# Two-layer sequence model on one core: attention's first queries and keys in other memory, four heads to a transfer, and one store moved to GpSimd's queue

## Chip, core and metric

The kernel runs on one core of a Trainium2 chip. The metric is the device time of one execution in microseconds (us), the median of several runs. Engines are named as the profile names them: PE (TensorE matmul), PEld (its weight load), DVE (VectorE), ACT (ScalarE), POOL (GpSimd), SP (SyncE, which here only issues transfers). "SPq", "ACTq" and "POOLq" are those engines issuing a transfer.

## What is computed

Input: 8 batches of 512 tokens, 256 wide, float32 throughout. Two layers, each a mixer and an expert feed-forward side by side on the normed input, added to the residual:

```python
x  = L0_attn_u                                   # [8, 512, 256]
xn = layernorm(x)
x  = x + state_space_mixer(xn) + moe_top1(xn)    # layer zero: 8 heads, chunks of 128; 8 experts
xn = layernorm(x)
x  = x + attention(xn) + moe_top2(xn)            # layer one
```

Layer one's attention has 16 heads of width 16 and keys and values that go through a latent of 64:

```python
q = x @ Wq;  latent = (x @ Wk + x @ Wv) @ W_down_kv
k_rec = latent @ W_up_k;  v_rec = latent @ W_up_v
scores = (q_h @ k_h.T) * scale * exp(-0.0001 * |i - j|)      # each batch, each head: 512 x 512
out = softmax(scores) @ v_h ; out @ Wo
```

Its feed-forward has 7 experts of capacity 512 and a "no-op" expert; tokens go to the best two.

## The kernel before

**Three stretches.** Layer zero's mixer goes through 64 chunks (`Chunk`, eight to a batch), with the batch's projections, convolutions and output (`Batch`) cut in pieces between them, and layer zero's experts and then layer one's preparation (`late`: norm, transposes, projections to q, k and v) threaded in by `fill`. Then layer one runs 128 attention steps (`Step`: batch b, group g of four heads, quarter c of the keys), with expert pieces between them. The third stretch, at the end, adds everything up. All instructions are written in a fixed order (`manual_schedule`); each engine runs its own list in order, and a transfer waits on the engine that issues it until what it needs is there, with all that stands behind it in that engine's list.

**The seam.** The last batch of layer zero ends with four calls of `Batch.output` (L1088 to L1102). For the last batch the sum goes into the tile `final` (taken from the tag `xr`), so that layer one can norm it without loading it again; after the fourth piece SP stores it to the DRAM array `x1` (L1100). The projections had put q and k of batches 0 to 6 in DRAM as `rows["q"]` and `rows["k"]`, 256 rows (16 heads of 16) by 512 tokens. In layer one's block, `spread` brings them back for batch 0: one tile of 128 partitions for each group of four heads, head i at partitions 32*i to 32*i+15, one transfer of 16 rows (32 KB) for each head. q goes through SP's queue, k through ACT's (L1728 to L1732); behind them SP loads `vt` (values) and `w_o`. POOL clears `low` and three tiles `wv` (L1739 to L1742). For batches 1 to 7, `inputs_of` (called at step (2,0) of the batch before) loads `vt` at once and puts the 32 transfers in the list `loads`, of which `load_some(6)` in each step hands six to SP.

A score step multiplies four heads at once: `s_ps` (L1580), four matmuls with 16 rows each in four row groups of the array, then DVE takes each through the decay band and its maximum (L1583, `s`), ACT takes the exponentials (L1593, L1597), and two steps later PE multiplies with the values (L1605, `o_ps`). The quotient of a pair of groups goes through DRAM (`divide`: stores `od`, loads `sm` and `oT`, store `rd`, load `rb`, then DVE multiplies at L1723), all on SP's queue. DVE also norms the last batch and builds the routing table of the last batches (`en_r`, `en_b`, `en_w`, L219 to L223), which PE sums up (`tab`, L231).

**Memory.** Tiles come from pools, and a pool from a stack; a tag's buffers lie side by side, and the tags of a pool follow one another in the order in which they are first asked for. Layer zero's pools are closed ahead of layer one's, and the framework puts in the waits that the reuse needs. In bytes of a partition:

| pool | from | to | what lies there |
|---|---|---|---|
| layer zero `m1` | 48608 | 79328 | z, states st0 (56800 to 58848) and st1, x, au, u (71136 and 75232, 4096 each) |
| layer zero `m2` | 79328 | 181920 | yT (79328 and 87520, 8192 each), bc (95712 and 103904, 8192 each), xT (112096 and 116192, 4096 each), the eight `row` buffers (from 120288), mt, fr, xdt and smaller ones |
| layer one `a1` | 53344 | 69440 | w_o, peaks, low (57440 to 57568), wv, rows, oT |
| layer one `a2`, before | 69440 | 132480 | vt (69440), qT (78144, six of 2048), kT (90432, six), s1 (102720, twelve of 2048), then ng, w, sm, fo and smaller ones |
| layer one `a2`, changed | 69440 | 132480 | s1 (69440, twelve), fo (94016, two of 1024), qT (96064, six), kT (108352, six), vt (120640), then the rest |

The tiles of the last batch in layer zero are the second buffers of yT (87520) and u (75232) and the first of bc (95712).

Of the kernel before, what the change touches and what calls it, by code (L numbers as in the profile page):

```python
# [9 lines left out]
FP = mybir.dt.float32  # L10
# [7 lines left out]
P = 128  # L18
B, S, DM = 8, 512, 256
NT = B * S  # L20
NTILE = NT // P
TPB = S // P
# [23 lines left out]
AH, AD, DL = 16, 16, 64  # L46
VH = AD + 1
VW = AH * VH
# [16 lines left out]
def tile_kernel(ctx: ExitStack, tc: tile.TileContext, t, out: bass.AP):  # L65
    nc = tc.nc
    V, A, G, T, Y = nc.vector, nc.scalar, nc.gpsimd, nc.tensor, nc.sync
# [7 lines left out]
    def load(name, shape, pool=None):  # L75
        w = ctile("w_" + name, shape, pool=pool)
        Y.dma_start(out=w, in_=t[name])
        return w
# [35 lines left out]
    x1 = dram.tile([NT, DM], FP, name="x1", tag="x1")  # L114
# [7 lines left out]
    def rows_of(src, b):  # L122
        return src[b * S : (b + 1) * S, :].rearrange("(c p) d -> p c d", p=P)
# [248 lines left out]
    def bank(name, shape, tag="gen"):  # L372
        return mp.tile(shape, FP, name=name, tag=("e", "s")[tag] if isinstance(tag, int) else tag, bufs=2)
# [194 lines left out]
    with ExitStack() as es:  # L568
        p1, p2, psum = m1, m2, mp
# [365 lines left out]
        class Batch:  # L935
# [152 lines left out]
            def output(self, c):  # L1088
                op = bank("op", [P, DM])
                for k in range(HC):  # L1090
                    T.matmul(  # L1091
                        op, self.yT[:, k, c * P : (c + 1) * P], w_out[:, k, :], start=(k == 0), stop=(k == HC - 1)
                    )

                def add():
                    x = self.u[:, c, :]
                    to = final[:, c, :] if self.b == B - 1 else x
                    V.scalar_tensor_tensor(to, op, self.rs[:, c : c + 1], x, ALU.mult, ALU.add)
                    if c == TPB - 1:
                        Y.dma_start(out=rows_of(x1, self.b), in_=final if self.b == B - 1 else self.u)  # L1100

                return add  # L1102

# [122 lines left out]
        with tc.manual_schedule(engines=ENGINES):  # L1226

            rows, rest, sizes = itertools.chain(route0(), blocks()), late(), step_sizes()
# [127 lines left out]
            final = tl.tile([P, TPB, DM], FP, name="xr", tag="xr", bufs=3)  # L1356
# [14 lines left out]
    with tc.tile_pool(name="a1", bufs=1) as p1, tc.tile_pool(name="a2", bufs=2) as p2, tc.tile_pool(  # L1371
        name="ap", bufs=1, space=PSUM
# [80 lines left out]
        def spread(rows, got, n, by=None):  # L1453

            for g in range(4):
                wide = p2.tile([P, S], FP, name=n + "T", tag=n + "T", bufs=6)
                for i in range(4):
                    h = 4 * g + i
                    to, of = wide[32 * i : 32 * i + AD, :], rows[h * AD : (h + 1) * AD, :]
                    if by:  # L1460
                        by.dma_start(out=to, in_=of)
                    else:
                        loads.append((to, of))
                got.append(wide)
# [3 lines left out]
        def load_some(k):  # L1468
            for to, of in loads[:k]:
                Y.dma_start(out=to, in_=of)  # L1470
            del loads[:k]

        def inputs_of(b):
            rows, vd = kept[b]
            got = {"q": [], "k": [], "v": p2.tile([P, TPB, VW], FP, name="vt", tag="vt")}
            Y.dma_start(out=got["v"], in_=vd)
            for n in ("q", "k"):
                spread(rows[n], got[n], n)
            return got
# [68 lines left out]
        def combine():  # L1548


            def add(b):
                G.dma_start(out=x_sb[:, b * TPB : (b + 1) * TPB, :], in_=rows_of(x1, b), accum_op=ALU.add)

            for b in (B - 1, *range(B - 2)):
                add(b)
            yield
            while B - 2 not in finished:
                yield
            add(B - 2)
            for b in range(B - 1):  # L1560
                G.dma_start(out=rows_of(out, b), in_=x_sb[:, b * TPB : (b + 1) * TPB, :])
# [164 lines left out]
                urgent.insert(0, finish(b, oT))  # L1726

        with tc.manual_schedule(engines=ENGINES):  # L1728
            rows, vd = kept[0]
            got = {"q": [], "k": [], "v": p2.tile([P, TPB, VW], FP, name="vt", tag="vt")}  # L1730
            spread(rows["q"], got["q"], "q", Y)
            spread(rows["k"], got["k"], "k", A)  # L1732
            Y.dma_start(out=got["v"], in_=vd)
            w_o = load("w_o", [P, KC, DM], p1)
            steps = [(b, g, c) for b in range(B) for g in range(4) for c in range(TPB)]
# [18 lines left out]
            rows, number1 = combine(), None  # L1754
# [45 lines left out]
            for n in range(N + 2):  # L1800

                if n < N:
                    b, g, c = steps[n]
                    if (g, c) == (2, 0) and b + 1 < B:
                        got = inputs_of(b + 1)
# [15 lines left out]
                    now.scratch = scratch  # L1821
                    done.append(now)
                    now.scores()
                load_some(6)
                for chain in list(chains):
                    if next(chain, "end") == "end":
                        chains.remove(chain)
# [117 lines left out]
def build(arrays):  # L1945
    import concourse.bacc as bacc

    nc = bacc.Bacc("TRN2", target_bir_lowering=False, num_devices=1)
    t = {
        k: nc.dram_tensor(f"in_{k}_dram", v.shape, mybir.dt.from_np(v.dtype), kind="ExternalInput").ap()  # L1950
        for k, v in arrays.items()
    }
    out = nc.dram_tensor("out_0_dram", (NT, DM), FP, kind="ExternalOutput").ap()
    with tile.TileContext(nc) as tc:
        tile_kernel(tc, t, out)
    return nc
# [10 lines left out]
```

## Time and profile before

| what | value |
|---|---|
| three runs | 1734.75 us median, 1732.07 to 1735.76 |
| the profiled execution | 1730.83 us, of which the span is 1729.1 us |
| PE busy | 1567.4 us (91%) |
| DVE busy | 1173.9 us (68%) |
| ACT busy | 916.3 us (53%) |
| POOL busy | 571.0 us (33%) |
| HBM traffic | 133 GB/s over the span |
| q and k loads, all batches | 256 transfers of 32 KB |

All times below are us from the span's start. In the chain of waits, a line is when a piece begins, how long it is on the chain, and what it is; in the timeline, a line is start, duration, engine, source line and what is written from what, with the idle time ahead of it and what ended that in brackets. In tables by stretch, each engine has its busy time, and PEclk is the TensorE clock that was granted, with 1.00 for full speed.

### The profile page before, as it was taken

To read this page: it belongs to the slowest core of one execution; us is meant where nothing else is said; L and a number is where in the kernel's file an instruction comes from. 1 tells how busy PE (TensorE), PEld (TensorE's weight loads), DVE (VectorE), ACT (ScalarE), POOL (GpSimd) and SP (SyncE) were. 2 spreads that over 40 slices of the span, in tenths; PEclk is the share of its full clock that TensorE was granted. 3 is DMA by queue.
4 is the path that set the end of the run, shared out by engine and by line. 5 is a ranking of instruction groups with operands and counts; after the bars stand their busy time and mean duration, and the time that the engine had idled before them with its cause. 6 is when DMAs were issued, how large, how long until landed. Compare 5 with 4: busy or idle time off the path is not lost.

```text
span 1729.1 us, 25738 instructions
## 1 busy us (share of the span) xinstructions
PE 1567.4 (91%) x8700; PEld 962.1 (56%) x8700; DVE 1173.9 (68%) x3067; ACT 916.3 (53%) x2173; POOL 571.0 (33%) x518
## 2 busy tenths in 40 slices
PE   6556799989999999999789898799999999999996
PEld 5323467767677677777445554564455445454442
DVE  6567675575576655875776925657777777777774
ACT  4232345345354453453544643327777777777773
POOL 0041456465465474654532422000211121112030
PEclk9777899999999999999989998759999999999986
DMA  8010445454564564564355624323433343344254
GB/s 295 21 55 0 152 159 198 161 187 180 166 212 146 175 196 148 181 221 137 83 115 163 179 87 145 105 74 114 135 86 111 97 133 97 90 119 141 57 98 125
DMA packets 131821, 231.09 MB, mean 134 GB/s; under 512 B 20109, under 2 KB 93839, under 8 KB 120528
## 3 DMA queue, kind: packets, MB, share of 16 engines
q1 hardware_dynamic: 101952, 119.46, 22.0%
q0 software_dynamic: 28656, 108.69, 20.6%
q8 instruction: 73, 1.20, 0.3%
q10 hardware_dynamic: 1072, 1.18, 0.3%
q14 instruction: 68, 0.56, 0.1%
HBM read 176.75 MB, written 53.58 MB: 133 GB/s over the span
## 4 chain that ended last, share of the span: by engine, by line
PE 71%; DVE 19%; ACT 4%; DMA 3%; issue 2%; POOL 0%; SPq 0%; ACTq 0%; DVEq 0%; POOLq 0%
PE s_ps L1580 7%; PE pj L946 7%; PE h_ps L640 7%; PE o_ps L1605 7%; PE y_ps L664 7%; PE e_hp L1423 5%; PE e_yp L1436 5%; DVE cv L959 3%; PE yd L1172 3%; PE op L1091 3%; PE seg L1134 3%; DVE s L1583 3%; PE sp L1202 2%; PE yoff L1190 2%; ACT s L1597 2%
## 5 line engine op out<-in xcount | busy, mean ns | idle before, releaser
L1583 DVE CUSTOM_DVE_ANT_0 s<-s_ps,band 128x512 f32<-128x512 f32 x512 | 323.1, 687 | 148.2 <-PE s_ps L1580 148.2
L1597 ACT ACTIVATE s<-s,ng 128x512 f32<-128x512 f32 x512 | 325.7, 708 | 0.0
L946 PE MATMUL pj<-xT,w_w_in 128*128 128x512 f32 x384 | 197.3, 640 | 9.5 <-DVE cv L959 5.5
L1441 POOL DMA_INDIRECT x<-e_yo,number x28 | 45.0, 1608 | 422.4 <-ACT e_yo L1440 342.2
L1580 PE MATMUL s_ps<-qT,kT 16*128 16x512 f32 x1024 | 166.7, 678 | 4.6 <-DMA kT<-kd 4.6
L959 DVE SCALAR_TENSOR_TENSOR cv<-pj,w_conv_w,cv 128x511 f32<-128x511 f32 (+2 forms) x192 | 143.2, 746 | 22.2 <-ACT cv L955 17.7
L1118 POOL TENSOR_TENSOR au<-da,half 128x512 f32<-128x512 f32 x64 | 76.6, 1197 | 228.7 <-PE seg L1134 156.7
L640 PEld LDWEIGHTS h_ps<-xdT,w 128*128 128x128 f32 x1152 | 138.8, 194 | 19.1 <-issue 18.3
L1605 PE MATMUL o_ps<-s,wv 128*32 128x512 f32 x1024 | 145.4, 640 | 1.2 <-ACT w L1593 1.2
L640 PE MATMUL h_ps<-xdT,w 128*128 128x128 f32 x1152 | 141.9, 277 | 0.5 <-DMA w<-in_w_dram,w_idx 0.5
L664 PE MATMUL y_ps<-w,hT 128*128 128x256 f32 x576 | 138.4, 384 | 0.0
L664 PEld LDWEIGHTS y_ps<-w,hT 128*128 128x128 f32 x576 | 108.3, 193 | 29.9 <-issue 16.1
L946 PEld LDWEIGHTS pj<-xT,w_w_in 128*128 128x128 f32 x384 | 69.8, 200 | 90.5 <-issue 80.1
L1580 PEld LDWEIGHTS s_ps<-qT,kT 16*128 16x128 f32 x1024 | 51.7, 193 | 119.0 <-DVE w L1590 51.1
L1423 PE MATMUL e_hp<-e_xdT,e_w 128*128 128x256 f32 x448 | 113.5, 391 | 3.7 <-ACT fo L1542 1.9
L1436 PE MATMUL e_yp<-e_w,e_hT 128*128 128x256 f32 x448 | 113.4, 392 | 1.5 <-ACT fo L1542 1.5
L1181 DVE TENSOR_TENSOR yT<-yT,yd 128x512 f32<-128x512 f32 (+1 forms) x64 | 43.8, 684 | 100.2 <-PE yd L1172 100.2
L1147 ACT ACTIVATE mt<-seg,mid 64x64 f32<-64x64 f32 x512 | 109.4, 309 | 0.8
L1436 PEld LDWEIGHTS e_yp<-e_w,e_hT 128*128 128x128 f32 x448 | 80.1, 189 | 50.6 <-issue 30.3
L1423 PEld LDWEIGHTS e_hp<-e_xdT,e_w 128*128 128x128 f32 x448 | 82.1, 191 | 40.8 <-ACT s L1597 15.2
L963 ACT ACTIVATE th<-cv 128x512 f32<-128x512 f32 x64 | 40.3, 630 | 116.7 <-DVE cv L959 108.0
L955 ACT ACTIVATE cv<-pj,w_conv_b,w_conv_w 128x512 f32<-128x512 f32 x64 | 49.8, 778 | 87.4 <-PE pj L946 83.4
(341 smaller groups left out, 2818.3 us busy)
## 6 DMA issues: line engine op xcount, KB each, us to landing
ex<-exd SPq DMA_DIRECT2D x96, 128.0 KB
fr<-fdd SPq DMA_DIRECT2D x64, 128.0 KB
e_w<-in_ei_dram SPq DMA_DIRECT2D x7, 1024.0 KB
od<-os SPq DMA_DIRECT2D x28, 256.0 KB
e_w<-in_eo_dram SPq DMA_DIRECT2D x7, 1024.0 KB
vd<-vt SPq DMA_DIRECT2D x16, 272.0 KB
vt<-vd SPq DMA_DIRECT2D x8, 544.0 KB
u<-in_u_dram SPq DMA_DIRECT2D x8, 512.0 KB
```

Source lines behind the costliest of these rows:

```text
L640: T.matmul(hp[:, i, :], w1[:, k * FF + f * P : k * FF + (f + 1) * P], xdT[:, k * P : (k + 1) * P], start=(k == 0), stop=(k == KC - 1),)
L664: T.matmul(yp, hT[f // 4][:, f % 4, :], w2[:, f * DM : (f + 1) * DM], start=(f == 0), stop=(f == FC - 1),)
L946: T.matmul(pj, w_in[:, k, o * P : (o + 1) * P], self.xT[:, k, :], start=(k == 0), stop=(k == KC - 1))
L959: V.scalar_tensor_tensor(cv[:, s:], pj[:, : S - s], conv_w[:, q, 3 - s : 4 - s], cv[:, s:], ALU.mult, ALU.add)
L1118: G.tensor_tensor(self.au, bc(da[:, d, self.i, :], 2, HH), bc(TRI[d], 1, HH), ALU.mult)
L1147: A.activation(mt[lo, over, h], seg[lo, over, h], AF.Exp, bias=mid[lo, self.i, h : h + 1])
L1423: T.matmul(hp, w1[:, k, f * P : (f + 1) * P], xdT[:, k, :], start=(k == 0), stop=(k == KC - 1))
L1436: T.matmul(yp, hT[:, f, c * P : (c + 1) * P], w2[:, f, :], start=(f == 0), stop=(f == FC - 1))
L1580: T.matmul(sp[i], self.k[r, cols], self.q[r, :], start=True, stop=True)
L1583: V.tensor_tensor_reduce(out=self.p[i], in0=sp[i], in1=band[:, at : at + S], scale=1.0, scalar=KEEP, op0=ALU.mult, op1=ALU.max, accum_out= ...
L1597: A.activation(self.p[i], self.p[i], AF.Exp, bias=self.ng[:, i : i + 1])
L1605: T.matmul(op[32 * i : 32 * i + 32, :], self.wv[:, i, :], self.p[i], start=(self.c == 0), stop=(self.c == TPB - 1),)
```

## The change

Three edits. `Batch.output` stores the last batch through POOL's queue instead of SP's. `spread` moves a group of four heads with one transfer: its source walks over 32 rows from each head's first, so that the upper 16 partitions of each strip receive rows of the next head, which no matmul reads; in the last group, where that would run past the array, one transfer moves three heads and another the fourth. That is 10 transfers a batch in place of 32, 256 KB each where they move four heads, 192 KB and 32 KB in the last group; `load_some` hands over two of them a step in place of six. Last, layer one's block asks for twelve tiles of `s1` and two of `fo`, unused, ahead of all others, and for `vt` behind q and k, so that the tags get the places of the table's last row.

```diff
@@ Batch.output, the last piece
-                        Y.dma_start(out=rows_of(x1, self.b), in_=final if self.b == B - 1 else self.u)
+                        if self.b == B - 1:
+                            G.dma_start(out=rows_of(x1, self.b), in_=final)
+                        else:
+                            Y.dma_start(out=rows_of(x1, self.b), in_=self.u)
@@ spread
-                for i in range(4):
-                    h = 4 * g + i
-                    to, of = wide[32 * i : 32 * i + AD, :], rows[h * AD : (h + 1) * AD, :]
+                strips = 4 if g < 3 else 3
+                of = bass.AP(
+                    tensor=rows.tensor, offset=rows.offset + 4 * g * AD * S, ap=[[AD * S, strips], [S, 32], [1, S]]
+                )
+                moves = [(wide[: 32 * strips, :], of)]
+                if strips < 4:
+                    moves.append((wide[96 : 96 + AD, :], rows[DM - AD :, :]))
+                for to, of in moves:
                     if by:
                         by.dma_start(out=to, in_=of)
                     else:
@@ layer one's block
+            for _ in range(12):
+                p2.tile([P, S], FP, name="s1", tag="s1", bufs=12)
+            for _ in range(2):
+                p2.tile([P, DM], FP, name="fo", tag="fo")
             rows, vd = kept[0]
-            got = {"q": [], "k": [], "v": p2.tile([P, TPB, VW], FP, name="vt", tag="vt")}
+            got = {"q": [], "k": []}
             spread(rows["q"], got["q"], "q", Y)
             spread(rows["k"], got["k"], "k", A)
+            got["v"] = p2.tile([P, TPB, VW], FP, name="vt", tag="vt")
             Y.dma_start(out=got["v"], in_=vd)
@@ each step
-                load_some(6)
+                load_some(2)
```

## Prediction

> **What bounds the kernel now.** I read the page's chain first, by engine:
>
> ```profile
> PE 71%; DVE 19%; ACT 4%; DMA 3%; issue 2%; POOL 0%; SPq 0%; ACTq 0%; DVEq 0%; POOLq 0%
> ```
>
> PE carries the end, and transfers hold only 3% of it. The change can pay only where the chain passes through one of its transfers, so I next read the chain in order of time around the seam:
>
> ```profile
> 1098.00 0.98 PE sm L1078 x8
> 1099.10 7.50 issue
> 1106.59 0.36 ACTq L1461
> 1106.99 3.58 DMA kT<-kd
> 1110.59 5.64 PE s_ps L1580 x13
> ...
> 1121.72 0.40 DVE en_w L223
> 1122.16 7.08 PE tab L231 x32
> ```
>
> A load of keys is on the chain for about 4 us. ("issue" for 7.50 us is not idleness: PE ran the 32 matmuls of the last output then, until 1105.99.) The timeline says what the load waited for and who waited behind it:
>
> ```profile
> 1106.03 0.48 DVE L1098 SCALAR_TENSOR_TENSOR xr<-op,rq_r,u 128x256 f32<-128x256 f32 x1 [0.56 <-PE op L1091]
> 1106.55 0.37 SPq L1100 DMA_DIRECT2D x<-xr  x1
> 1106.59 10.16 ACTq L1461 DMA_DIRECT2D kT<-kd  x16
> 1106.63 0.12 POOL L1739 MEMSET low<- 128x32 f32 x1 [16.42 <-DVE xr L1098]
> 1107.08 9.99 SPq L1461 DMA_DIRECT2D qT<-qd  x16
> 1110.59 6.85 PE L1580 MATMUL s_ps<-qT,kT 16*128 16x512 f32 x16 [4.59 <-DMA kT<-kd]
> 1112.66 0.69 DVE L1583 CUSTOM_DVE_ANT_0 s<-s_ps,band 128x512 f32<-128x512 f32 x1 [5.47 <-PE s_ps L1580]
> 1116.80 0.20 ACT L1593 ACTIVATE w<-w 128x4 f32<-128x4 f32 x1 [17.70 <-DMA kT<-kd]
> ```
>
> The last add of layer zero ends at 1106.51. Within 0.12 us of it three queues come free: SP's store, ACT's first k load, POOL's clearing of `low`. Then all of PE, DVE and ACT wait for the first q and k. The rest of layer one I read by stretches and by the waits of 1200 to 1660:
>
> ```profile
> 1108.50:1110.00 1.50, 0.00 (x0) 0.00 (x0) 0.00 (x0) 0.00 (x0) 0.00 (x0) 0.50 0.86 260
> 1200.00:1600.00 400.00, 396.89 (x2348) 197.96 (x2340) 295.05 (x1080) 306.49 (x634) 64.48 (x48) 1.00 0.38 112
> PE e_hp L1423 <- ACT fo L1542: 1.9, 7, 0.5
> DVE s L1583 <- PE s_ps L1580: 113.0, 99, 3.2
> DVE oT L1723 <- DMA rb<-rd: 2.1, 2, 1.3
> ```
>
> From 1200 to 1600 PE idles 3.1 us in 400, and none of it is charged to q or k; DVE idles on PE. Loads of later batches are hidden.
>
> **Edit one, the memory.** What it could bring: in the old places qT begins inside u's second buffer and kT inside yT's, both used until the very end; in the new ones they lie over bc and xT, last read by PE at 1082.70 (yoff) and about 1084.9 (the last z projection). ACT's list is free from 1099.09 (end of L286) and SP's from about 1099.7. If waits went by bytes, q and k would land before PE's last output matmul.
>
> I don't expect it, because of `low`. It lies at 57440, over state st0, which PE last read (yoff) by 1082.70; no other layer-zero tile shares those bytes. Yet POOL, idle for 16.42 us, was let go by the add that reads `u`, 17 KB further up in the same pool. So reuse is not waited for byte by byte but pool by pool. The program's own waits say the same: its first k transfer waits for the load and the accumulation into `u` and for ACT's copy L1073 into a `row` buffer, none of which shares a byte with it. The edit leaves qT and kT in pool `a2`, which reaches over `m1` and `m2` before and after alike. The last user of both is that add. So ACT's first k load still goes at 1106.59, and SP's first q load, now without the store ahead of it, at about 1106.6. Gain: 0.
>
> **Edit two, four heads to a transfer, first batch.** SP's 16 issues and ACT's 16 become 5 each. What decides is when the first group has landed. Nearest row: rb, 256 KB into 128 partitions, issued alone at 1205.20, let DVE start at 1209.28, 4.08 us later.
>
> ```profile
> 1205.20 0.61 SPq L1720 DMA_DIRECT2D rb<-rd  x1
> 1209.28 0.69 DVE L1723 TENSOR_TENSOR oT<-oT,rb 128x512 f32<-128x512 f32 x1 [1.33 <-DMA rb<-rd]
> ```
>
> That gives 1106.59 + 4.08 = 1110.67, against 1110.59: +0.1. From above: if the second 256 KB (k beside q) came wholly after the first, at the 260 GB/s of the stretch above, 1.0 us more: +1.1. From below: rd, 16 KB, took 3.18 us on the chain (1202.00), so 1106.59 + 3.2 = 1109.8: -0.8; the 512 KB store no longer runs ahead of q on SP's queue, which speaks for that side. I take +0.1. After that four heads are there at once, where before they dripped in every 0.6 us; but DVE started 2.07 us after the first matmul before, and at half clock a step with all four heads there takes the same (s_ps x8 at 1129.17, DVE at 1131.28: 2.11). From 1112.66 on DVE runs without a gap through eight scores, the norm's small steps and the table to 1122.12, and PE's `tab` waits for that. So the path moves by what the first landing moves: +0.1, between -0.8 and +1.1.
>
> ACT does get free sooner: its issuing ended at 1116.75, while its first `w` was ready at about 1115.6 (L1590). So about 1 us on ACT, and the norm of the last batch (L740, 1121.90) about 1 us sooner. Who waits for ACT? PE's transposes of that norm at 1138.87 stand behind `tab` in PE's list, 15 us later; the first gather of expert rows goes at 1158.4. On the path: 0. SP too is done 5 to 6 us sooner, with `vt` first used at 1130.62: 0.
>
> **Edit two, later batches.** SP issues 10 transfers instead of 32, which took 19 us a batch in five pieces (12 in 9.22, 4 in 1.77, 2 in 0.88, 6 in 2.78, 8 in 4.39). The cover is the lead: loads are handed over in steps (2,0) to (3,0), and the next batch begins three steps, about 12 us, later. Bytes double to 2 MB a batch, about 13 GB/s more on 112 GB/s. Upper bound of a gain: PE's 3.1 us of idleness. Upper bound of a loss: the slower rival below. I take 0.
>
> **Edit three, the store on POOL.** POOL pays 1.30 us for such a transfer (the 512 KB row L701 at 1056.46: 1299 ns) ahead of `low` and `wv` (0.62 us), so `wv` is clear at about 1108.5; its first use is at 1130.62. Queued behind it on POOL is nothing until the gather at 1158.4. POOL's 512 KB rows land after 5.8 to 13.8 us (medians of three groups), so the store has read `final` by 1112.4 to 1120.4; L740, which overwrites `final`, came at 1121.90. Cover 0.5 us at worst, and a lateness there has the 15 us above. 0.
>
> A page of the Trainium skill speaks against this edit (DMA: Bandwidth & Descriptors, Specifications): simple stores belong on Sync, with a first byte after about 0.6 us, against 1 us from GpSimd. The rows here are harsher (1.30 us of POOL against 0.37 us of SP), and by either the sum stays, since nobody waits for that store.
>
> **Sum**, on the profiled execution: 1730.83 + 0.1 + 0 + 0 + 0 = 1730.9, which lies 3.9 us below the median of the runs shown. On the median: 1734.8. About 0.2% (3.5 us) is what a measurement of this kernel can tell from no change.
>
> **Rivals.** *The memory does come free sooner* (waits go by bytes for these tiles). Then scores start when the last add has left its PSUM bank, 1106.51, and DVE 1.16 us later (full-clock rows 1221.88 to 1223.04): 1107.7 instead of 1112.66, 5.0 us off the path: 1729.8. For it: the new places fit exactly past yT's end (95712). Against: `low`. Chance 0.08. The half clock would not go with the gap: granted 1.00 until 1108.5, it is 0.50 from there to 1159.5, and the DVE-bound pause ahead of `tab` (PE idle 1117.4 to 1122.16) would still be there. The Trainium skill (TensorE: Matmul & The Clock Gate, HAM oscillation) asks for no PE pause over 3.4 us; by that rule too the pause ahead of `tab` would throttle it, and the sum is the same.
>
> *Fewer waits on PE pay.* The score line has these on its weight side:
>
> ```profile
> L1580 PEldq EVENT_SEMAPHORE  x85: 51/51/51, 1215.9 to 1649.8; - x85
> ```
>
> 85 x 51 ns = 4.3 us; if all stood on the path and went, 1730.4. Against: PE's idleness is 3.1 us and 3.4 us of waits are put down to `fo`. Chance 0.07.
>
> *Slower: big loads ahead of the quotient's small transfers.* In steps (2,0) to (3,0) SP now sends up to 512 KB a step where it sent 192 KB; 320 KB more at 260 GB/s is 1.2 us, ahead of each of od, sm/oT and rd/rb of the batch's second group. If two of the three hops feel it, L1723 comes 2.4 us later in each of 7 batches; DVE's slack on PE is about 1.0 us a step (113.0 us over some 115 steps), so 1.4 x 7 = 9.8 us: 1744.6. It decides as soon as a hop loses more than 1 us. For it: two of 14 already waited, 1.3 us at most. Against: SP's issue time in those steps shrinks from about 2.7 to 0.9 us. Chance 0.13.
>
> **How the numbers follow.** No change worth the name: 0.72, at 1734.8. Its own range is -0.8 to +1.1 of the landing, and about 2 us each way for the spread of the runs shown: 1732 to 1738. To take in the two faster rivals and a fifth of the slower one the range is 1729.5 to 1739.5. Faster by over 0.2%: 0.08 + 0.05 (most of the PE rival) + 0.01 = 0.14. Slower: 0.13 + 0.02 = 0.15. Within: 0.71.
>
> **What would show it.** Right: ACT's first kT issue within 0.2 us after the last L1098; PE's first score 3 to 5.5 us after that; ACT's first `w` about 1 us sooner; PE busy 99% from 1200 to 1600. Wrong: kT issued at about 1099 while PE still does `op` (the first rival); waits of L1723 on rb grown from 2.1 us to 10 or more (the slower one); L740 waiting on POOL's store.

## The result, and the profile after

The changed kernel takes 1754.20 us (median of six runs, 1742.81 to 1763.82) against 1730.01 for the kernel before in the same runs (1724.62 to 1735.76). The ratio is 1.0123, with a 95% interval of 1.0092 to 1.0155: slower by some 21 us, where no difference had been forecast. The profiled execution took 1752.04 us (span 1750.3) against 1730.83 (span 1729.1): 21.2 us between the spans.

Transfers now hold 4% of the chain, against 3%. In order of time, its pieces that are transfers (start, length on the chain, what):

```profile
1100.08 13.02 DMA qT<-qd
...
1206.77 7.79 DMA rd<-sm
1214.58 3.45 DMA rb<-rd
```

The load of the first q and k, 3.58 us on the chain before, is now 13.02. The two transfers of the quotient, `rd` (16 KB) and `rb` (256 KB), were on the chain before too, once:

```profile
1202.00 3.18 DMA rd<-sm
...
1205.20 3.98 DMA rb<-rd
```

Here `rd` has grown by 4.6 us, and the pair comes a second time, in the next batch (from 1279.73, with 6.87 and 4.01 us). The timeline of the changed kernel around the seam says when the loads went and who waited:

```profile
1099.41 8.69 SPq L1469 DMA_DIRECT2D qT<-qd  x5
1099.41 13.88 ACTq L1469 DMA_DIRECT2D kT<-kd  x5
...
1113.36 2.09 PE L1588 MATMUL s_ps<-qT,kT 16*128 16x512 f32 x8 [14.54 <-DMA qT<-qd]
1118.28 0.20 ACT L1601 ACTIVATE w<-w 128x4 f32<-128x4 f32 x1 [26.36 <-DVE w L1598]
```

The last add of layer zero ended at 1099.33 in this execution, so the loads went within 0.1 us of it, as before. The first score came 13.95 us after the issue; PE's pause is 14.54 us, against 4.59. And by stretches (PE, PEld, DVE, ACT and POOL busy, then the granted clock, the mean busy share of the 16 DMA engines, and GB/s):

```profile
1107.00:1111.00 4.00, 0.00 (x0) 0.00 (x0) 0.00 (x0) 0.00 (x0) 0.00 (x0) 0.50 0.28 106
...
1200.00:1300.00 100.00, 95.99 (x539) 47.86 (x541) 69.05 (x256) 70.92 (x145) 16.44 (x12) 0.97 0.41 122
```

While every compute engine stood still and over 1 MB of q and k was still to come, the DMA engines were about a quarter busy, at 106 GB/s; the kernel before moved 260 GB/s in this place at a share of 0.86. A quarter of 16 is 4, and 4 is the outermost dimension of the new source, `[[AD * S, strips], [S, 32], [1, S]]`. From 1200 to 1300 PE was busy 95.99 us, against 99.64 before, and its clock fell to 0.97. The waits of 1200 to 1660 (who, for what: us in total, times, longest; the second line is SyncE's queue) name the place:

```profile
DVE oT L1731 <- DMA rb<-rd: 17.1, 6, 4.3
...
SPq L1728 <- DMA rd<-sm: 46.5, 13, 7.4
```

Before, these were 2.1 us in 2 waits and 16.9 in 14.

The 21.2 us split by events on DVE: from the end of layer zero's last add to the first step's `ng` (DVE's negated peaks, one a step) it is 18.7 us against 8.8; from there to batch 1's first `ng` 112.4 against 106.3; batches 1 to 6 take 429.0 against 416.8; the rest 90.9 against 90.6. That is +9.9, +6.1, +12.2 and +0.3 (of batch 0's 6.1 us, 3.1 are there by its step 8, under the half clock, and 3.0 come at its end, where `rb` is late), and layer zero, which the change doesn't touch, ended 7.2 us sooner in this execution.

### The profile page after: what moved, and what is told of

Its sections match the earlier page's. It is cut to its first block, busy times and chain, and to the rows that moved or that the text cites. A ratio compares the mean times of both kernels' runs of the same rounds, so it can differ in the third digit from the quotient of the medians.

```text
span 1750.3 us, 25486 instructions
## 1 busy us (share of the span) xinstructions
PE 1575.3 (90%) x8700; PEld 963.2 (55%) x8700; DVE 1172.7 (67%) x3067; ACT 917.1 (52%) x2173; POOL 575.8 (33%) x519
## 3 DMA queue, kind: packets, MB, share of 16 engines
q10 hardware_dynamic: 1087, 1.67, 0.3%
## 4 chain that ended last, share of the span: by engine, by line
PE 70%; DVE 19%; ACT 4%; DMA 4%; issue 2%; POOL 0%; SPq 0%; DVEq 0%; POOLq 0%; ACTq 0%
PE pj L946 7%; PE s_ps L1588 7%; PE h_ps L640 7%; PE o_ps L1613 7%; PE y_ps L664 7%; PE e_hp L1426 6%; PE e_yp L1439 4%; PE op L1091 3%; DVE s L1591 3%; PE seg L1137 3%; DVE cv L959 3%; PE yd L1175 3%; PE sp L1205 2%; PE yoff L1193 2%; ACT s L1605 2%
## 5 line engine op out<-in xcount | busy, mean ns | idle before, releaser
L1588 PE MATMUL s_ps<-qT,kT 16*128 16x512 f32 x1024 | 174.6, 680 | 15.3 <-DMA qT<-qd 14.5
L959 DVE SCALAR_TENSOR_TENSOR cv<-pj,w_conv_w,cv 128x511 f32<-128x511 f32 (+2 forms) x192 | 143.2, 746 | 20.3 <-ACT cv L955 15.8
L640 PEld LDWEIGHTS h_ps<-xdT,w 128*128 128x128 f32 x1152 | 140.0, 195 | 19.2 <-issue 18.4
```

Of the source, the lines that this page charges most:

```text
L640: T.matmul(hp[:, i, :], w1[:, k * FF + f * P : k * FF + (f + 1) * P], xdT[:, k * P : (k + 1) * P], start=(k == 0), stop=(k == KC - 1),)
L959: V.scalar_tensor_tensor(cv[:, s:], pj[:, : S - s], conv_w[:, q, 3 - s : 4 - s], cv[:, s:], ALU.mult, ALU.add)
L1588: T.matmul(sp[i], self.k[r, cols], self.q[r, :], start=True, stop=True)
```

## The experiments

**The theory** was that the outermost dimension of the source sets how many DMA engines a transfer runs on: 4 of them, in all the wide loads. **The rivals**: the new places or the store on GpSimd's queue cost the time; or the doubled bytes, in SyncE's queue ahead of small transfers, do, as the recorded prediction's slower rival has it. Ratios are to the kernel before on the same chip, with 95% intervals. Expected times in us go by 1730 for the kernel before; it took 1733.5 to 1734.9 in the runs beside most experiments, so the ratios say more.

**Without the wide loads.** One head per transfer everywhere, everything else as changed.

```diff
-                strips = 4 if g < 3 else 3
-                of = bass.AP(...)
-                moves = [(wide[: 32 * strips, :], of)]
-                ...
+                moves = [
+                    (wide[32 * i : 32 * i + AD, :], rows[(4 * g + i) * AD : (4 * g + i + 1) * AD, :]) for i in range(4)
+                ]
...
-                load_some(2)
+                load_some(6)
```

> The changed kernel with its q and k loads taken back to one head each (16 rows, 32 KB, 16 issues per queue at the seam, six handed over per step later). What is left of the change: the new places in memory and the last store on GpSimd's queue. Theory (the loss comes from transfers whose source has an outermost dimension of 4 and which run on 4 of the 16 DMA engines): nothing is left that loses, 1730 us, within 3; PE's pause before its first score 4 to 5 us, waits of DVE on rb about 2 us in all. Rival one (the new places in memory or the store from GpSimd's queue cost the time): about 1750. The recorded reasoning also says that the first k load still goes only after the last add of layer zero, since reuse is waited for pool by pool: issue within 0.2 us after that add.

Measured: 1731.95 us, 0.9979 (0.9950 to 1.0008). DVE's waits on rb are 2.2 us in all. Its timeline:

```profile
1108.70 1.90 PE L1584 MATMUL s_ps<-qT,kT 16*128 16x512 f32 x4 [3.22 <-DMA qT<-qd]
```

No loss is left, so places and store don't cost it. The first loads went at 1106.08, with the last add's end (1106.00). PE's pause fell from 4.59 to 3.22 us, under what was expected, with the store no longer ahead of q, but DVE's first `ng` came 8.6 us after the last add, against 8.8.

**Wide loads in the first batch alone, and in the later ones alone.** The first batch is the one that passes `by`. For the second kernel the two sides change places, and `load_some(2)` stays.

```diff
+                if by:
                     moves = [(wide[: 32 * strips, :], of)]
                     ...
+                else:
+                    moves = [... one head each ...]
...
-                load_some(2)
+                load_some(6)
```

> The changed kernel with four heads per transfer in the first batch only; later batches load one head at a time. Theory of the few engines: the pause of PE before its first score stays at 13 to 15 us (4.6 before), the rest of layer one is as before: 1739 to 1743 us. Rival one (memory or store): about 1750, as the whole change. Rival two (the doubled bytes in later batches stand in SP's queue ahead of small transfers, and the seam's loss is made up for later): 1730 to 1733.

> The changed kernel with four heads per transfer in batches 1 to 7 only; the first batch loads one head at a time. Theory of the few engines: PE's pause before its first score is back at 4 to 5 us, but rd and rb of the quotient still wait up to 7 us each in some steps, since a transfer spread over all engines ends only when its part on the busy engines ends: 1740 to 1748 us, with DVE's waits on rb at 10 to 25 us in all. If nearly the whole loss comes from the seam: 1730 to 1735.

Measured: first batch alone 1742.33 us, 1.0050 (1.0026 to 1.0074); later batches alone 1749.73 us, 1.0089 (1.0057 to 1.0120). PE's pause in the first is 14.51 us. The waits on rb in the second:

```profile
DVE oT L1736 <- DMA rb<-rd: 18.7, 6, 4.8
```

Both halves lose, the later batches more. The second's 1749.73 us lie 2 us above the expected range; by the ratio (1.0089 of 1730 is 1745) it is inside.

**Same bytes, an outermost dimension of 32.** Each head's 32 rows as a transfer of its own: the bytes of the change, but an outermost dimension of 32.

```diff
+                for i in range(4):
+                    h = 4 * g + i
+                    n_rows = 32 if h < AH - 1 else AD
+                    moves.append((wide[32 * i : 32 * i + n_rows, :], rows[h * AD : h * AD + n_rows, :]))
...
-                load_some(2)
+                load_some(8)
```

> The changed kernel with its bytes kept, but each head's 32 rows (64 KB) as a transfer of its own, so that the outermost dimension is 32; 16 issues per queue at the seam, eight handed over per step later. Bytes per step, order in SP's queue and places are those of the changed kernel; only the outermost dimension and the number of issues differ. Theory of the few engines: first score 4 to 7 us after the first issue, DVE's waits on rb at most 5 us in all, 1729 to 1735 us. Rival two (twice the bytes ahead of the quotient's small transfers in SP's queue): DVE's waits on rb 10 us or more and 1740 to 1750 us.

Measured: 1741.41 us, 1.0040 (1.0018 to 1.0063), between the two theories by the ratio, and inside the rival's range in us. The first score came 2.6 us after the issue, sooner still than the theory of the engines has it, but DVE waited 11.2 us on rb, as the rival has it. The timeline shows a third cause, which is in this kernel alone:

```profile
1202.24 5.18 SPq L1476 DMA_DIRECT2D kT<-kd  x8
1203.16 0.35 DVE L1723 RECIPROCAL sm<-sm 128x32 f32<-128x32 f32 x1
1207.53 0.36 SPq L1724 DMA_DIRECT2D rd<-sm  x1
```

`sm` was ready at 1203.51, but SyncE was still issuing eight transfers, and `rd` went 4.0 us late. So this run's time doesn't tell bytes from engines for the later batches: it added an issue cost that the change doesn't have (there `rd` was issued at once, at 1206.77, and landed 7.8 us later). What `rd` took once it was issued does speak. Each batch has two quotients: the first falls among the loads of the next batch, the second where no q or k load is in flight. From issue to the issue of `rb`, the first ones of batches 0 to 6 took 2.1 to 3.2 us in the kernel before, 5.0 to 7.8 in the changed one, and 1.5 to 3.4 here, with the same bytes in the same queue. The next run leaves the issue cost out.

**Eight engines.** The same single transfer, bytes, order and places, but the source written as 8 blocks of 16 rows; every second block brings other rows that nobody reads (6 blocks in the last group).

```diff
-ap=[[AD * S, strips], [S, 32], [1, S]]
+ap=[[AD // 2 * S, 2 * strips], [S, AD], [1, S]]
```

> The changed kernel with the source of its wide loads written with an outermost dimension of 8 (blocks of 16 rows, every second one holding rows that nobody reads; 6 in the last group) in place of 4. Bytes, number of transfers, queues and places stay. Theory (rate goes with the number of engines, 24.5 GB/s each): about 196 GB/s between 1105 and 1118 where the changed kernel had 98; first score 6 to 9 us after the first issue (14.5 with 4, 3.2 with one head each); waits on rb between the 11.2 us of the kernel with 32 rows per head and the 17.1 us of the changed kernel; time 1.005 to 1.009 of before. Rival (bytes and order alone, however many engines): first score as late as in the changed kernel, 1.012.

Measured: 1741.58 us, 1.0031 (0.9999 to 1.0063). A stretch of its seam, and its waits of 1200 to 1660:

```profile
1119.00:1123.00 4.00, 1.40 (x8) 0.55 (x8) 0.00 (x0) 0.00 (x0) 0.00 (x0) 0.50 0.54 201
```

```profile
DVE oT L1731 <- DMA rb<-rd: 1.7, 2, 1.4
```

The share is a half, the rate 201 GB/s, and the first score came 9.3 us after the issue, a little later than expected. The time is under what was expected, since batches 1 to 6 lose nothing at all: they take 416.6 us (416.8 before), and the 11 us or more of waits on rb were not found. The doubled bytes are free there.

**Two engines, first batch alone.** Two heads per transfer; later batches one head each.

```diff
-ap=[[AD * S, strips], [S, 32], [1, S]]
+ap=[[AD * S, 2], [S, 32], [1, S]]
...
-moves = [(wide[: 32 * strips, :], of)]
+moves.append((wide[64 * j : 64 * j + 64, :], of))
```

> As the kernel with wide loads in the first batch alone, but two heads per transfer, so that the outermost dimension is 2; later batches one head at a time. Theory (the number of engines sets the rate): 49 GB/s at the seam in place of 98, first score 22 to 28 us after the first issue, total some 8 to 14 us above the kernel with 4 in the first batch: 1.010 to 1.014 of before. Rival (the size of the piece that must land before work can begin): the pieces are half as large, so the first score comes sooner than with 4, 8 to 10 us after the issue, and 1.001 to 1.003.

Measured: 1753.69 us, 1.0122 (1.0086 to 1.0158). A stretch of the seam:

```profile
1114.00:1122.00 8.00, 0.03 (x2) 0.06 (x2) 0.00 (x0) 0.00 (x0) 0.00 (x0) 0.55 0.13 51
```

An eighth of the engines and 51 GB/s, as the theory says. The first score was not as late as expected, 11.9 us after the issue and not 22 or more, since a piece holds two heads; but the four heads of the first step were through DVE only 20.3 us after the last add, against 18.6 with four engines. The ratio lies 12 us above that kernel; the profiled executions show 3 of these behind the last add, and the rest is open. So share and rate go with the dimension (0.13, 0.28, 0.54 and 51, 106, 201 GB/s for 2, 4 and 8). The Trainium skill has this rule (DMA: Bandwidth & Descriptors, Why a DMA increments its semaphore by 16 and not by 1): the engines used are the largest number up to 16 that divides the outermost dimension, other than 1, of both sides. The three shares agree with it.

**The later loads from another queue.** The whole change, still 4 engines, but `load_some` issues on GpSimd.

```diff
             for to, of in loads[:k]:
-                Y.dma_start(out=to, in_=of)
+                G.dma_start(out=to, in_=of)
```

> The changed kernel with the q and k loads of batches 1 to 7 issued from GpSimd's queue in place of SyncE's; still 4 heads per transfer, an outermost dimension of 4 and the same bytes in the same steps. Theory one (rd and rb wait for the few busy engines, whatever queue filled them): waits on rb stay at 10 to 20 us, 1.009 to 1.013 of before. Theory two (rd and rb wait because they stand behind the wide loads in SyncE's own queue): waits on rb fall to 2 to 4 us and the time to that of the kernel with wide loads in the first batch alone, 1.004 to 1.006.

Measured: 1742.70 us, 1.0055 (1.0031 to 1.0079), the time of the kernel with wide loads in the first batch alone; DVE waited 1.0 us on rb. That looks like theory two, but the trace takes it back. `rd` of the first pair went at 1213.31 and had landed by 1214.73; before it, this stretch:

```profile
1202.00:1206.00 4.00, 4.00 (x25) 1.92 (x26) 2.91 (x12) 3.18 (x8) 0.00 (x0) 1.00 0.00 0
```

Nothing was moving. GpSimd had issued its loads earlier and in a bunch, and the engines were 0.54 busy from 1193 to 1201 and 0.75 from 1261 to 1277, more than four can be. The Trainium skill has a place for that too (DMA: Bandwidth & Descriptors, Why a DMA increments its semaphore by 16 and not by 1): from GpSimd's queue a transfer of k engines takes k neighbours that move on from transfer to transfer, from SyncE's and ACT's the lowest k. So this run changed three things, queue, moment and engines, and tells nothing apart. Three more do.

**The quotient's transfers from another queue.** The wide loads stay where they are.

```diff
-            Y.dma_start(out=rd[8 * j : 8 * j + 8, :].rearrange("h (p f) -> (h p) f", f=32), in_=sm)
+            G.dma_start(out=rd[8 * j : 8 * j + 8, :].rearrange("h (p f) -> (h p) f", f=32), in_=sm)
...
-            Y.dma_start(out=rb, in_=bc(rd[8 * j : 8 * j + 8, :], 1, [8, AD, S]))
+            G.dma_start(out=rb, in_=bc(rd[8 * j : 8 * j + 8, :], 1, [8, AD, S]))
```

> The whole changed kernel (wide loads of 4 engines, on SyncE's queue, in the same steps), but rd and rb, the two small transfers of the quotient, are issued from GpSimd's queue. Theory one (rd stands behind the wide loads in SyncE's own queue): with wide loads in flight rd now lands in 2 to 4 us, DVE's waits on rb are at most 5 us in all, and the time is that of wide loads in the first batch alone, 1.004 to 1.007 of before. Theory two (rd's share on the four busy engines is late whatever queue it came from): rd lands in 5 to 8 us, waits on rb 10 to 20 us, 1.009 to 1.013.

Measured: 1758.44 us, 1.0157 (1.0125 to 1.0189). Its timeline, and the stretch between:

```profile
1210.12 0.59 POOL L1726 DMA_DIRECT2D rd<-sm  x1 [40.68 <-DVE wv L1609]
1215.13 0.68 POOL L1728 DMA_DIRECT2D rb<-rd  x1 [4.42 <-DMA rd<-sm]
```

```profile
1210.00:1215.00 5.00, 5.00 (x36) 2.51 (x29) 3.86 (x14) 4.13 (x9) 0.59 (x1) 1.00 0.29 109
```

From a queue with no wide load in it, `rd` still took 5.0 us (4.9 to 5.5 in the seven first quotients up to batch 6), while the DMA share was 0.29 at 109 GB/s, and DVE waited 21.4 us on rb in all. Part of that is GpSimd's queue itself: in the second quotients, with no wide load in flight, `rd` took 2.4 to 3.7 us from it, and once 5.8, where SyncE's took 1.4 in the changed kernel. So this run alone doesn't clear SyncE's queue; the next one does it better. It agrees with the Trainium skill's rule that spreading transfers over queues gives no more bandwidth, since all run on the same engines (DMA: Bandwidth & Descriptors, Rules for kernel authors).

**The later loads from ACT.** The mirror image, in `load_some`: now SyncE's queue, with `rd` and `rb` in it, has no wide load.

```diff
-                Y.dma_start(out=to, in_=of)
+                A.dma_start(out=to, in_=of)
```

> The whole changed kernel, but the q and k loads of batches 1 to 7 are issued from ACT's queue, in the same steps and still with an outermost dimension of 4. Unlike GpSimd's, this queue is of the same kind as SyncE's. Theory one (place in SyncE's queue): waits on rb at most 5 us, rd landing in 2 to 4 us while wide loads are in flight; ACT pays for ten issues a batch, so 1.004 to 1.010 of before. Theory two (busy engines): waits on rb 10 to 20 us and 1.009 or more.

Measured: 1777.76 us, 1.0261 (1.0235 to 1.0287), the slowest of all. Its timeline:

```profile
1216.91 0.32 SPq L1726 DMA_DIRECT2D rd<-sm  x1
...
1222.23 0.61 SPq L1728 DMA_DIRECT2D rb<-rd  x1
```

DVE waited 17.7 us on rb, as in the changed kernel, with SyncE's queue free of wide loads. `rd` took 5.3 us here and 5.0 to 5.7 in all seven first quotients, from the same queue that brings it in 2.1 to 3.2 in the kernel before. A place behind the wide loads in SyncE's queue is therefore not needed for the delay; the 6.9 and 7.8 us of the changed kernel's first two may hold some of it. Above the waits on rb come 17.9 us on `sm`, and an ACT that issues beside its own work; which of these makes the rest of the loss wasn't tried.

**One wide load a step.** Engines, queue and bytes as changed, at half the pace.

```diff
-                load_some(2)
+                load_some(1)
```

> The whole changed kernel, but one wide load handed over per step in place of two (load_some(1)); four engines, SyncE's queue and bytes stay. Theory (a backlog on the four engines holds rd and rb): 256 KB a step take 2.6 us at 100 GB/s where a step lasts about 4.3, so no backlog builds up; rd lands at most 2.6 us later than before, DVE's waits on rb are 2 to 8 us in all, batches 1 to 6 take 417 to 421 us, and the time is 1.004 to 1.008 of before (the seam's loss stays). Rival (any wide load of four engines in the later batches costs, whenever it goes): batches 1 to 6 at 427 to 433 us and 1.010 to 1.014.

Measured: 1738.16 us, 1.0029 (1.0006 to 1.0051), a little less than expected, and in the waits of 1200 to 1660:

```profile
DVE oT L1731 <- DMA rb<-rd: 1.5, 1, 1.5
```

Batches 1 to 6 take 416.6 us: nothing is lost there, with the same four engines and the same bytes. So it is the backlog. Two wide loads a step, 512 KB, take about 5 us at the 106 GB/s of four engines, and a step takes 4.3 (416.8 / 96), so the four fall behind. That `rd` then waits for its own part on those four is the reading that fits all these runs; no row shows single engines.

**Reuse waited for tile by tile.** The recorded reasoning had it that the new places bring nothing because a pool's memory is waited for as a whole. The two pools of layer one can be opened otherwise:

```diff
-tc.tile_pool(name="a1", bufs=1) as p1, tc.tile_pool(name="a2", bufs=2) as p2
+tc.tile_pool(name="a1", bufs=1, reuse_waits="tile") as p1, tc.tile_pool(name="a2", bufs=2, reuse_waits="tile") as p2
```

First with the new places, the store on GpSimd and one head per transfer:

> The new places in memory and the store on GpSimd's queue, q and k loaded one head at a time as before, and the two pools of layer one that hold q, k and the small tiles opened so that each tile waits only for the tiles whose bytes it takes, not for whole pools. Theory (the new places bring nothing in the change because reuse is waited for pool by pool): the first k load is issued some 7 us before the last add of layer zero, PE's pause before its first score falls from 3.2 us (run with one head each) or 4.6 us (before) to 0.5 to 1 us, and the time is 1726 to 1731 us, 2 to 5 us under the kernel with the same loads and pool waits (0.9979 of before), so 0.995 to 0.997. Rival (the seam is held by something else, the score banks or the queues): pause and time as in that kernel.

Measured: 1725.29 us, 0.9957 (0.9930 to 0.9984), the one version whose interval lies wholly under 1. Its timeline:

```profile
1097.39 0.36 ACTq L1465 DMA_DIRECT2D kT<-kd  x1
...
1099.09 8.56 SPq L1465 DMA_DIRECT2D qT<-qd  x16
1105.32 0.48 DVE L1098 SCALAR_TENSOR_TENSOR xr<-op,rq_r,u 128x256 f32<-128x256 f32 x1 [0.56 <-PE op L1091]
1105.90 1.47 PE L1584 MATMUL s_ps<-qT,kT 16*128 16x512 f32 x8 [0.62 <-issue]
```

The loads now run under the last output matmuls, 8.4 us ahead of the last add's end, and PE starts the scores 0.1 us after that. Is it the waits alone? The kernel before with them, and the same with the store moved as well:

> The kernel before, old places, store on SyncE's queue, one head per transfer, with the waits of the two pools tile by tile and nothing else. Theory (SyncE's store, which waits for the last add, stands ahead of the q loads in SyncE's list): k loads go early, but the first q load still goes after the last add; PE's pause before its first score 2.5 to 3.5 us in place of 4.6, 0.998 to 1.000 of before. Rival (tile waits alone are the gain of 0.9957): pause under 1 us and 0.994 to 0.997.

> The kernel before with the last store moved to GpSimd's queue and waits tile by tile; old places, one head per transfer. If the new places are needed (q and k of the old places lie over tiles that layer zero uses to its end): some q or k transfer of the first group still waits for the last of layer zero and PE's pause stays at 2.5 us or more, 0.998 to 1.000. If the order of the queue was all, and the places are not needed: pause under 1 us, 0.994 to 0.997, as with the new places.

Measured: 0.9991 (0.9964 to 1.0019) and 0.9991 (0.9970 to 1.0012). The second one's timeline:

```profile
1109.32 9.81 ACTq L1464 DMA_DIRECT2D kT<-kd  x16
1109.78 9.56 SPq L1464 DMA_DIRECT2D qT<-qd  x16
```

The last add began at 1109.27, when PE had done its last matmul, and ended at 1109.75. In the old places k goes with the one and q with the other. In the first of the two k went with the last add as well, at 1114.19, and not early as I had expected; PE waited 4.09 us, not 2.5 to 3.5. So places (0.9979, from 0.9950 to 1.0008, in the first experiment) and waits show no sure gain alone, and 0.4% together. The intervals overlap; what sets the version with both apart is its first `ng`, 3.8 us after the last add, against 8.6, 7.7 and 7.9.

Last, wide loads of eight engines with these waits, in all batches and in the later ones alone:

> Wide loads with an outermost dimension of 8 in all batches, the new places, the store on GpSimd's queue, and waits for reused memory tile by tile. Theory: the first k load goes at about 1097.4, the first q load at 1099.1; what took 9.9 us from issue to first score with pool waits now starts some 7 us sooner, so PE's pause before its first score is 2 to 4 us, and the later batches lose nothing: 0.997 to 1.000 of before. Rival (at 8 engines the transfers of the seam also slow the work before it, or land as late): 1.002 or more.

> New places, store on GpSimd's queue, waits tile by tile; the first batch one head per transfer, later batches in wide loads with an outermost dimension of 8. Theory: the seam is that of the 0.9957 kernel and the later loads are hidden in either form: 0.994 to 0.997, the same as that kernel within 0.2%. Rival (fewer transfers in later batches bring a gain of their own, in PE's waits on semaphores or SyncE's time): 0.993 or less.

Measured: 0.9996 (0.9968 to 1.0024) and 0.9975 (0.9950 to 1.0000). In all batches, the first q and k needed longer than the 8 us that were hidden, and PE still waited 2.75 us. In the later batches alone the ratio can't be told from that of one head everywhere; fewer transfers bring no further gain.

All runs by stretches, in us of the profiled execution: the end of layer zero's last add, from there to the first `ng`, from that to batch 1's first, batches 1 to 6, and the rest.

| kernel | last add | to first `ng` | batch 0 | batches 1 to 6 | rest | ratio |
|---|---|---|---|---|---|---|
| before | 1106.5 | 8.8 | 106.3 | 416.8 | 90.6 | 1 |
| changed | 1099.3 | 18.7 | 112.4 | 429.0 | 90.9 | 1.0123 |
| one head everywhere | 1106.0 | 8.6 | 109.0 | 416.8 | 92.2 | 0.9979 |
| wide in the first batch | 1110.6 | 18.6 | 109.5 | 416.6 | 94.6 | 1.0050 |
| wide in later batches | 1105.3 | 8.4 | 115.5 | 432.2 | 88.6 | 1.0089 |
| one head of 32 rows | 1106.9 | 9.1 | 114.7 | 418.6 | 90.5 | 1.0040 |
| eight engines | 1112.3 | 14.0 | 108.7 | 416.6 | 92.6 | 1.0031 |
| two engines, first batch | 1110.0 | 20.3 | 112.6 | 416.6 | 92.9 | 1.0122 |
| later loads on GpSimd | 1106.1 | 18.7 | 108.5 | 417.1 | 91.4 | 1.0055 |
| quotient on GpSimd | 1102.6 | 18.6 | 112.6 | 431.0 | 88.1 | 1.0157 |
| later loads on ACT | 1104.7 | 18.4 | 116.7 | 451.7 | 89.7 | 1.0261 |
| one wide load a step | 1117.8 | 17.6 | 109.0 | 416.6 | 88.3 | 1.0029 |
| one head, tile waits | 1105.8 | 3.8 | 108.5 | 416.6 | 92.6 | 0.9957 |
| eight engines, tile waits | 1106.7 | 6.9 | 109.5 | 416.6 | 94.7 | 0.9996 |
| old places, tile waits | 1114.6 | 7.7 | 108.5 | 416.6 | 89.2 | 0.9991 |
| the same, store on GpSimd | 1109.8 | 7.9 | 103.6 | 416.9 | 90.1 | 0.9991 |
| one head first, eight engines later | 1099.4 | 3.8 | 104.2 | 416.6 | 92.7 | 0.9975 |

## Why the prediction was wrong

**Edit one, the memory: right, and for the reason given.** The first k load went within 0.1 us of the last add, and opening the pools with waits by tile let it go 8.4 us ahead. The rival that has the memory free sooner was priced at 5.0 us off the path; when the runs made it true, the first `ng` came 5.0 us sooner after the last add (3.8 against 8.8).

**Edit two, first batch: wrong, and here the prediction failed first.** The step that failed is the landing of the first group. It took 4.08 us from rb's row, "256 KB into 128 partitions", which compares bytes and partitions, and its upper bound took 260 GB/s from a stretch with a DMA share of 0.86. The term that was missing is the source's outermost dimension. From issue to first score it was 13.95 us, against a range of 3.2 to 5.1; the sum's +0.1 was +9.9 by the first `ng`. The diff shows the dimension, and the prediction doesn't mention it; rb's own source, `bc(rd[8 * j : 8 * j + 8, :], 1, [8, AD, S])`, begins with 8, and not with 4. Nor was rb issued alone, as the prediction says: eight loads of k followed 0.66 us behind it. Nor is 13.95 only two transfers of 256 KB at 100 GB/s, which make 5.2 us. The queues of the changed kernel from 1103 to 1105 (packets, MB, share) show why:

```profile
q1 hardware_dynamic: 69, 0.14, 22.9%
q0 software_dynamic: 6, 0.02, 3.0%
```

SyncE's q and a rest of GpSimd's store moved, but nothing of ACT's k, which had been issued at the same time as q. By packets of 2 KB, 128 to a transfer, the first q moved until about 1105.6, with GpSimd's store at 0.73 to 0.78 of the engines' time from 1101.0 to 1102.2; k's first packets moved at 1105.0, when the first q was nearly through, then beside the second, and its 128 were through by about 1111.3. So the waits add up; some 2 us from there to 1113.1, where the chain ends the wait, are not accounted for. Why k's transfer held back wasn't tried, nor was the store's part with wide loads.

**ACT's issuing: wrong size, right effect.** It was to shrink and grew, from 10.16 us to 13.88 for 5 transfers instead of 16. On the path it is still 0: ACT's first `w` waited for DVE, not for its own issues.

**Edit two, later batches: the cover named was the wrong one.** The sum's 0 was +12.2 us in batches 1 to 6 of the profiled execution. "The lead" did hide the loads themselves: no wait of 1200 to 1660 is charged to q or k. It doesn't hide what else uses those engines. The rival pointed at the right victims, `rd` and `rb`, for the wrong reason. Bytes at 260 GB/s in SyncE's queue was its mechanism, at 9.8 us; but the same bytes in the same queue were free with eight engines, and `rd` was late (5.0 to 5.7 us) with the wide loads in ACT's queue. Against it stood that SyncE's issue time shrinks: true, `rd` was issued on time, and of no help. In the first of seven, `rd` took 7.79 us where it had taken 3.18. The ratios put the later batches at 1.0089 - 0.9979 = 1.1%, some 19 us, and the first batch at 1.0050 - 0.9979 = 0.7%; the whole change stands 1.4% over the same kernel, so the two don't simply add. It is the first batch's missing term again, not counted a second time. That the slower rival named the right victims was a good guess at 0.13, not a working.

**The clock was in no term of that sum.** After a long wait of DVE on rb, PE ran dry for 1.67 us and then was slow (changed kernel, stretches):

```profile
1290.00:1292.00 2.00, 0.33 (x5) 0.19 (x8) 1.30 (x3) 0.93 (x3) 1.06 (x1) 1.00 0.87 218
...
1296.00:1298.00 2.00, 2.00 (x6) 1.64 (x6) 1.20 (x7) 0.94 (x2) 0.00 (x0) 0.50 0.47 147
```

By the starts of `ng` against the kernel before, the batch boundary with this pause cost 6.4 us, and the five behind it 0.6 to 1.7 each. With wide loads in the later batches alone three boundaries cost 5.2 to 6.3 us, each with 6.8 us of half clock in it, two of them in batches 1 to 6, which is how that kernel lost more there (432.2 us) than the whole change (429.0). The first boundary shows both sides: 6.3 us there, where the clock fell, and 3.0 in the changed kernel, where PE paused for 1.98 us and the clock stayed at 1.00. So the length of PE's pause alone didn't say whether the clock fell. The seam's half clock also lasted 61.4 us, against 51.2.

**Edit three, the store: 0, as said.** With waits by tile in the old places the ratio is 0.9991 with it and without it. POOL paid 0.80 us, not 1.30.

**Fewer waits on PE: nothing.** The weight side's semaphore waits in the score line fell from 85 to 27, in the changed kernel and with eight engines alike; with eight engines, batches 1 to 6 took 416.6 us, against 416.8.

**Slips that decide nothing.** DVE's slack was shared out over some 115 steps, where 107 begin in that stretch (1.06 us a step); the doubled bytes are 14 to 15 GB/s more, not 13; and the chance of no change is given as 0.72 and as 0.71.

**What the spans owe to the clock.** Of the 3.1 us under the half clock, 2.8 are in the kernel with one head everywhere too. Batch 0 took 103.6 to 109.5 us in kernels whose later loads cost nothing and whose first pieces were not the slowest, and that doesn't follow the edits. It goes with a second, short stretch of half clock, which began some 12 to 14 us after the seam's had ended: with none (old places with the store on GpSimd; one head first) batch 0 took 103.6 and 104.2 us, with 6.8 us of it (before) 106.3, with 10.2 us (the others of these) 108.5 to 109.5. So does the rest: 88.1 to 89.2 us with 29 to 33 us of half clock in it, 89.7 to 91.4 with 36 to 39, 92.2 to 94.7 with 45 to 48. Single spans can't be compared to better than some 5 us for this reason. For the ratio 0.9957, some 7 us, the seam accounts for 5.0. In that kernel's profiled execution batch 0 and the rest are longer than before by 2.2 and 1.9, with more half clock in both (10.2 against 6.8, 45 against 39), so that from the last add to the end only 1.0 us of the gain is left there. Where the other 2 us of the ratio come from, and what sets these stretches, stays open.

## What to carry to other kernels

Before merging transfers, write down the outermost dimension of both sides of the new one: it, and neither bytes nor partitions, decided here what share of the 16 DMA engines worked, and a DMA share of a quarter with work queued is how that shows in a profile. A load that is hidden is not yet free: ask whether its engines keep up with the pace at which it is handed over, since a small transfer waited for the backlog here, whether the loads went through its own queue or ACT's. And an edit that brings nothing may lack a second one: new places and finer waits showed no sure gain alone, and 0.4% together.

## What the runs showed of the hardware that was not expected

In the kernel before, too, `rd` landed in 1.4 to 1.5 us in the second quotients, with no q or k load in flight, against 2.1 to 3.2 in the first ones: which suggests that even there a part of the hop is waiting for other transfers. Five issues on ACT took 13.88 us with four engines a transfer and 9.20 with eight, sixteen of the small ones 10.55: an issue waits where transfers are backed up, so that fewer issues need not free the engine sooner. The half clock came in fixed lengths: every stretch of it from the seam on, in all 17 traces and but for the last at each end, lasted a multiple of 3.41 us to within 0.1 (6.8 at the late boundaries, 44.4, 47.8, 51.2, 54.6, 58.0, 61.4 or 68.3 at the seam), so a small shift of work may cost or save a whole step. And layer zero, which is the same in all, ended between 1099.3 and 1117.8 us in these profiled executions, nearly the whole effect under study; only ratios over several runs, and events counted from the last add, could be compared.
